# A four-layer graph network on one core: three small transposes taken from the TensorE stream to DMA, transposes of the first and last graphs taken the other way, two layers scheduled a round later

## The chip, the cores and the metric

The kernel runs on one core of a Trainium2 chip. The metric is the device time of one execution in microseconds (us), from the first instruction to the last. The kernel before takes 2822.43 us, the median of 3 runs (2820.94 to 2826.75). In the profile PE is TensorE's matmul, PEld its weight load, DVE is VectorE, ACT is ScalarE, POOL is GpSimd and SP is SyncE, whose queue issues all DMA here.

## The reference

There are 64 graphs of 256 nodes with 256 features, all in float32. Each graph goes through four layers, each followed by `x = layernorm(x + layer(x, adj))`; the graphs don't touch each other.

```python
# layer 0: 4 heads of 64, sigmoid attention, normed by degrees
att = sigmoid(einsum('bhxd,bhyd->bhxy', q, k) * scale)
adj_h = adj_matrix[:, None] * att
deg = sum(adj_h, axis=-1)
dis = where(deg > 0, deg ** (-0.5), 0.0)
A = dis[..., :, None] * adj_h * dis[..., None, :]
Y = layernorm(A @ X) * ln_g + ln_b
# layer 1: 8 heads of 32, softmax attention masked by adj > 0
out = (softmax(where(adj > 0, q @ k.T / sqrt(HD), NEG)) @ v) @ Wo + bo
# layer 2: agg = epsilon * x + adjacency @ x; hidden width 1024
h = agg @ W1 + b1
h = silu(h * rsqrt(mean(h ** 2) + eps) * rms_weight)
out = h @ W2 + b2
# layer 3: additive attention
e = leaky_relu(s1[:, :, None] + s2[:, None, :], 0.2)      # s1 = Wh @ a1, s2 = Wh @ a2
h_prime = softmax(where(adj > 0, e, NEG)) @ Wh
out = gelu(layernorm(h_prime) * gamma + beta)
```

## The kernel before

A graph's 256 nodes are two blocks of 128 partitions. `graph` (L238) lists the operations of one graph through all four layers, each with an engine, a cost in ns, what it reads and what it writes; nothing is issued there. `Plan.order` (L94) then lays the operations of all 64 graphs out in one order for the five engines: it keeps a clock for each engine, takes the operation that can start earliest (ties go to the one due first) and gives out tile slots as it goes. `emit` (L714) issues them in that order, so the order on each engine is fixed beforehand, and each engine works its own list in order.

Several graphs are in flight at once. `turn` (L249) gives every ACT function that needs a table (sigmoid, exp, silu, gelu) a place: layer l of graph b belongs to round b + ROUND[l], with ROUND = 0, 2, 5, 7 (L31). The last graphs are cut off at the last graph's number, 63, plus TAIL[l], with TAIL = 0, 2, 3, 5 (L32). An operation with a turn may not go before its turn; loads may go up to AHEAD = 14 quarter rounds (L29) before they are due. All other operations may go as soon as they are ready. Tiles are of six kinds with fixed numbers of slots (SLOTS, L33): "s" is half a K words in each partition in SBUF, "c" a small SBUF tile, "p" a PSUM bank, "h" a scratch buffer in DRAM.

Transposes are done in two ways. `transpose` and `transposed` (L258, L266) use PE against an identity: four 128x128 transposes into PSUM, followed by a copy on ACT (`copy`, L297). `far_transposed` (L271) uses DVE for the 32x32 blocks and two DMA hops through a DRAM scratch ("far") to put the blocks in place. The large ones already go through DRAM: layer 1's exponentials, two heads at a time (L521 transposes blocks, L523 writes, L525 reads them back as eT in four parts), layer 0's result yT (L478) and layer 3's input xT3 (L628). PE does x1 and layer 3's e (L492, L656).

Three small transposes are done by PE, each as two 128x128 transposes into PSUM:

- L457, layer 0: the degrees. L449 puts the sums of the four heads in rows, ACT copies them (L452), and L457 turns them so that a partition holds its own node's degrees. DVE and POOL make `dis` of them (L461 to L463), which scales v (L467) and later y (L482).
- L606, layer 2: 1/rms. L601 (POOL) leaves one number to a node in a column; L606 turns it into a row repeated on all partitions, which eight DVE operations (L609) multiply into the hidden layer.
- L646, layer 3: the source terms s2, a column of v3, turned into a row repeated on all partitions, which the two Prelu of L650 (ACT) read. L646 carries layer 3's turn for exp.

Of the kernel before, what the change touches and what calls it, by code (L numbers as in the profile page):

```python
# [11 lines left out]
OP = mybir.AluOpType  # L12
# [13 lines left out]
DMA_KB, DMA_SEEN = 4, 1900  # L26

WORDS = {"s": 516, "d": 1024, "b": 2048, "c": 32, "p": 512, "h": 1024}
AHEAD = 14  # L29

ROUND = 0, 2, 5, 7  # L31
TAIL = 0, 2, 3, 5  # L32
SLOTS = {"s": 42, "d": 10, "b": 3, "c": 72, "p": 8, "h": 8}  # L33


# [39 lines left out]
class Plan:  # L75
# [9 lines left out]
    def op(self, engine, cost, fn, w=(), r=(), turn=None, mode="full", after=None, size=0):  # L85
        pair = lambda x: x if isinstance(x, tuple) else (x, None)
        w, r = [pair(x) for x in w], [pair(x) for x in r]
        op = Op(engine, cost, fn, w, r, self.graph, turn, mode, after, size)
        op.table = turn is not None and engine == "ACT"
        if op.table:  # L90
            self.turns[turn] = self.turns.get(turn, 0) + 1
        self.ops.append(op)
# [145 lines left out]
def graph(plan, nc, c, t, out, b):  # L238
# [10 lines left out]
    def turn(layer, func):  # L249
        return 4 * min(b + ROUND[layer], plan.graphs - 1 + TAIL[layer]) + func  # L250
# [20 lines left out]
    def far_transposed(src, name, in_order=True):  # L271


        eb, far, dst = Value("s", "eb"), Value("h", "far", 4), Value("s", name, 4)
        op("DVE", 635, lambda: dve.transpose(
            eb.t.rearrange("p (b g i) -> p g b i", b=4, i=32),
            src.t.rearrange("p (n k w) -> p k n w", n=2, k=2)), [eb], [src])
        if in_order:
            F = lambda a: far.t[:64].rearrange("(a z) (y w) -> a (z y) w", a=4, w=P)[a]
            for a in range(4):  # L280
                op("SP", 420, lambda a=a: nc.sync.dma_start(
                    F(a).rearrange("(b j) w -> j b w", b=4),
                    eb.t[32 * a:32 * a + 32].rearrange("j (b w) -> j b w", b=4)), [(far, a)], [eb], after=3000, size=64)
            for a in range(4):
                op("SP", 420, lambda a=a: nc.sync.dma_start(
                    dst.t.rearrange("q (g a i) -> a q g i", g=4, a=4)[a],
                    F(a).rearrange("q (g i) -> q g i", g=4)), [(dst, a)], [(far, a)], after=4500, size=200)
            return dst
        op("SP", 420, lambda: nc.sync.dma_start(far.t[:, :512], eb.t), [(far, i) for i in range(4)], [eb], after=3000, size=256)
        for q in range(4):  # L290
            op("SP", 420, lambda q=q: nc.sync.dma_start(
                dst.t[32 * q:32 * q + 32].rearrange("j (a g) -> j a g", a=4),
                far.t[:, :512].rearrange("(a j) (b g) -> b j a g", a=4, b=4)[q]), [(dst, q)],
                [(far, i) for i in range(4)], after=4200, size=64)
        return dst

    def copy(ps, name):  # L297
        dst = Value("s", name, 2)
        op("ACT", 466, lambda: act.copy(dst.t, ps.t), [dst], [ps])  # L299
        return dst  # L300
# [126 lines left out]
    def fn(pss=pss):  # L427
        for hp in range(H0 // 2):
            for m in range(NB):
                for i in range(2):  # L430
                    s = slice(i * HD0, (i + 1) * HD0)
                    pe.matmul(two(pss[2 * hp + i])[:, m, :], two(kT)[s, hp, m * P:(m + 1) * P], two(qT)[s, hp, :],  # L432
                              start=True, stop=True)
# [16 lines left out]
    op("PE", PE_MM, fn, [ps], added, mode="columns")  # L450
    deg = Value("s", "deg")
    op("ACT", 258, lambda ps=ps: act.copy(deg.t[:, :N], ps.t[:, :N]), [deg], [ps])  # L452
    pd = Value("p", "ps")

    def fn():
        for n in range(NB):
            pe.transpose(pd.t[:, n * P:(n + 1) * P], deg.t[:, n * P:(n + 1) * P], c.ident)  # L457
    op("PE", 2 * PE_TR, fn, [pd], [deg], mode="transpose")
    dp, dis = Value("c", "dp"), Value("c", "dis")
    D8 = lambda: pd.t[:, :N].rearrange("p (g k) -> p g k", k=32)[:, :, 0]  # L460
    op("DVE", 50, lambda: dve.tensor_scalar(dp.t[:, :8], D8(), TINY, None, op0=OP.max), [dp], [pd])  # L461
    op("POOL", 1610, lambda: pool.tensor_tensor(dp.t[:, :8], dp.t[:, :8], c.mhalf, OP.pow), [dp], [dp])  # L462
    op("DVE", 83, lambda: dve.scalar_tensor_tensor(dis.t[:, :8], D8(), 0.0, dp.t[:, :8], op0=OP.is_gt, op1=OP.mult),  # L463
# [11 lines left out]
                    pe.matmul(two(ps)[i * HD0:(i + 1) * HD0, hp, :], two(v)[:, m, h * HD0:(h + 1) * HD0],  # L475
                              A(h)[:, m, :], start=(m == 0), stop=(m == NB - 1))
    op("PE", 4 * PE_MM, fn, [ps], [v, att], mode="columns")
    yb = far_transposed(ps, "yT", in_order=False)  # L478
    y = Value("s", "y", 2)
    for i in range(2):  # L480
        by = lambda ap, i=i: ap.rearrange("p g (i k w) -> p g i k w", i=2, k=2)[:, :, i]
        op("DVE", 345, lambda y=y, i=i, by=by: dve.tensor_tensor(  # L482
            by(y.t.rearrange("p (g d) -> p g d", g=4)), yb.t.rearrange("p (i k g w) -> p i g k w", i=2, k=2, g=4)[:, i],
            dis.t[:, :8].rearrange("p (g i) -> p i g", i=2)[:, i, :, None, None].to_broadcast([P, 4, 2, 32]), OP.mult),
            [y], [yb, dis])
    mv, m = stats(y)
    affine(y, mv, m, c.g0, lambda n, xb=xb: two(xb)[:, n, :], [xb])
    x = normed(y, "x1")
# [14 lines left out]
    for hq in range(H1 // 4):  # L503
        pss = [Value("p", "ps", 2) for _ in range(4)]

        def fn(hq=hq, pss=pss):
            for n in range(NB):
                for i in range(4):
                    s = slice(i * HD1, (i + 1) * HD1)
                    pe.matmul(two(pss[i])[:, n, :], two(qT1)[s, hq, n * P:(n + 1) * P], two(kT1)[s, hq, :],  # L510
                              start=True, stop=True)
        op("PE", 2 * PE_MM, fn, pss, [qT1, kT1], turn=turn(1, EXP), mode="rows")
        for pair in range(2):


            e, eb, far, eT = Value("d", "e", 4), Value("d", "eb"), Value("h", "far"), Value("d", "eT", 4)
            for i in range(2):
                softmax(pss[2 * pair + i], negmask, HD1 ** -0.5, e,
                        lambda n, i=i, e=e: e.t[:, 256 * (2 * i + n):256 * (2 * i + n + 1)],
                        lambda n, i=i: 2 * i + n, r, lambda n, h=4 * hq + 2 * pair + i: 2 * h + n, turn(1, EXP))  # L520
            op("DVE", 1155, lambda e=e, eb=eb: dve.transpose(eb.t.rearrange("p (b g i) -> p g b i", b=4, i=32),  # L521
                                                             e.t.rearrange("p (g b i) -> p g b i", b=4, i=32)), [eb], [e])
            op("SP", 420, lambda eb=eb, far=far: nc.sync.dma_start(far.t, eb.t), [far], [eb], after=3500, size=512)  # L523
            for q in range(4):
                op("SP", 420, lambda far=far, eT=eT, q=q: nc.sync.dma_start(  # L525
                    eT.t[32 * q:32 * q + 32].rearrange("j (a g) -> j a g", a=4),
                    far.t.rearrange("(a j) (b g) -> b j a g", a=4, b=4)[q]), [(eT, q)], [far], after=4000, size=128)
            eTs.append(eT)


    def fn():
        for hq in range(H1 // 4):
            for m in range(NB):
                for i in range(4):
                    h = 4 * hq + i
                    pe.matmul(two(av)[i * HD1:(i + 1) * HD1, hq, :], two(v1)[:, m, h * HD1:(h + 1) * HD1],  # L536
                              eTs[h // 2].t.rearrange("p (a h n k i) -> p h k n a i", a=4, h=2, n=2, k=2)[:, i % 2, m],
                              start=(m == 0), stop=(m == NB - 1))
    op("PE", 4 * PE_MM, fn, [av], [v1, *eTs], mode="columns")

    op("DVE", 180, lambda: dve.reciprocal(r.t[:, :16], r.t[:, :16]), [r], [r])
    ps = Value("p", "ps")
# [56 lines left out]
    rs = Value("c", "rs")  # L599
    op("DVE", 50, lambda ps=ps: dve.tensor_scalar(rs.t[:, :NB], ps.t[:, :NB], 1e-6, None, op0=OP.add), [rs], [ps])  # L600
    op("POOL", 700, lambda: pool.tensor_tensor(rs.t[:, :NB], rs.t[:, :NB], c.mhalf[:, :NB], OP.pow), [rs], [rs])  # L601
    pr = Value("p", "pr")

    def fn():
        for n in range(NB):
            pe.transpose(pr.t[:, n * P:(n + 1) * P], rs.t[:, n:n + 1].to_broadcast([P, P]), c.ident)  # L606
    op("PE", 2 * PE_TR, fn, [pr], [rs], mode="transpose")
    for j in range(HB):
        op("DVE", 391, lambda j=j: dve.scalar_tensor_tensor(  # L609
            Hb(j)[:, 0], Hb(j)[:, 0], c.r2.t[:, j:j + 1], pr.t[:, :N], op0=OP.mult, op1=OP.mult), [(hT, j)], [(hT, j), pr, c.r2])  # L610
# [14 lines left out]
    x = normed(plus(ps, xb), "x3")  # L625


    xT3 = far_transposed(x, "xT3")  # L628
    v3 = Value("s", "v3", 2)
    V3 = lambda: v3.full.rearrange("p (n c) -> p n c", n=2)  # L630
    s1 = lambda n: V3()[:, n, D:D + 1]
    for n in range(NB):
# [6 lines left out]
        op("PE", 2 * PE_MM + 4, fn, [ps], [xT3, c.w3])  # L639

        op("ACT", 260, lambda ps=ps, n=n: act.copy(V3()[:, n, :], ps.t[:, :D + 2]), [(v3, n)], [ps])
    ps2 = Value("p", "ps2")

    def fn():
        for n in range(NB):
            pe.transpose(ps2.t[:, n * P:(n + 1) * P], V3()[:, n, D + 1:D + 2].to_broadcast([P, P]), c.ident)  # L646
    op("PE", 2 * PE_TR, fn, [ps2], [v3], turn=turn(3, EXP), mode="transpose")
    e = Value("s", "e3", 2)
    for n in range(NB):
        op("ACT", 360, lambda n=n: act.activation(two(e)[:, n, :], ps2.t[:, :N], AF.Prelu, bias=s1(n), alpha=0.2),  # L650
           [(e, n)], [ps2, v3])
    negmask = masked(load("adj3", "adj"))
    r3 = Value("c", "r3")
    softmax(e, negmask, 1.0, e, lambda n: two(e)[:, n, :], lambda n: n, r3, lambda n: n, turn(3, EXP))
# [96 lines left out]
```

## Time and profile before

| engine | busy us | share of the span | instructions |
|---|---|---|---|
| PE | 2752.3 | 97% | 17092 |
| PEld | 2189.6 | 78% | 17092 |
| DVE | 2494.3 | 88% | 7757 |
| ACT | 2131.5 | 75% | 5054 |
| POOL | 585.8 | 21% | 902 |

The profiled span is 2823.4 us. The chain that ended last lies on PE for 87% of it, on DVE for 5%, ACT 3%, DMA 2%. The 16 DMA engines are busy for 59.2% with the queue that SP feeds, and move 479.40 MB in all. A busy time is the union of the records of an engine; a mean in ns is the length of one record. Records of PE overlap, so the time that an instruction takes from the stream is read from start to start in the timeline. A matmul of 128x256 in float32 is two instructions, a transpose is one.

### The profile page before, as it was taken

Reading aid. Unit: us, or ns where it says so; the run is one execution under the profiler, and the core shown is the slowest. Engines: PE = TensorE matmul, PEld = TensorE weight load, DVE = VectorE, ACT = ScalarE, POOL = GpSimd, SP = SyncE. Lnnn points to the kernel's source line nnn. Section 1 sums busy time; section 2 is a strip of 40 time slices with the busy share of each in tenths; the row PEclk is TensorE's granted clock in tenths of the full one; section 3 lists DMA queues with packets and bytes.
Section 4 is the critical chain, followed back from the end, with each engine's and each line's share of the span. In section 5 each row is a group of like instructions: output and inputs, shape, how many; then the busy total and the mean of one; then the engine's idle time right before and its main releaser. Section 6 shows DMA issues by size and latency. Waiting matters only on the chain.

```text
span 2823.4 us, 55149 instructions
## 1 busy us (share of the span) xinstructions
PE 2752.3 (97%) x17092; PEld 2189.6 (78%) x17092; DVE 2494.3 (88%) x7757; ACT 2131.5 (75%) x5054; POOL 585.8 (21%) x902
## 2 busy tenths in 40 slices
PE   8899999999999999999999999999999999999996
PEld 6667777887787878788878878778787778777784
DVE  5788898989899998998899989899989989899975
ACT  3767787778688777877777777878768877686774
POOL 1011211212222222212212212222212221212111
PEclk9999999999999999999999999999999999999998
DMA  4857476646466646665576556556556647475641
GB/s 142 252 151 196 152 202 180 187 134 192 127 193 199 197 135 200 192 179 148 155 192 180 172 163 183 171 167 187 174 149 183 198 141 201 125 194 153 181 123 41
DMA packets 558613, 479.40 MB, mean 170 GB/s; under 512 B 184304, under 2 KB 516976, under 8 KB 558320
## 3 DMA queue, kind: packets, MB, share of 16 engines
q1 hardware_dynamic: 558320, 475.87, 59.2%
q8 instruction: 137, 2.24, 0.4%
q14 instruction: 156, 1.28, 0.2%
HBM read 290.60 MB, written 185.07 MB: 168 GB/s over the span
## 4 chain that ended last, share of the span: by engine, by line
PE 87%; DVE 5%; ACT 3%; DMA 2%; SPq 1%; issue 1%; POOL 0%; DVEq 0%; POOLq 0%; ACTq 0%
PE ps L622 15%; PE ps L308 15%; PE ps L319 14%; PE ps L579 14%; PE ps L510 4%; PE ps L432 4%; PE ps L567 4%; PE ps L637 4%; PE ps L475 3%; PE av L536 3%; PE ps L263 2%; ACT e L400 1%; PE ps L449 1%; DVE e L395 1%; DVE st L333 1%
## 5 line engine op out<-in xcount | busy, mean ns | idle before, releaser
L400 ACT ACTIVATE e<-e,low 128x256 f32<-128x256 f32 x1152 | 575.7, 501 | 73.5 <-DVE low L395 69.8
L622 PE MATMUL ps<-w,hT 128*128 128x256 f32 x2048 | 480.6, 382 | 4.2 <-ACT hT L613 4.2
L579 PE MATMUL ps<-aggT,w 128*128 128x256 f32 x2048 | 470.8, 382 | 2.8 <-ACT aggT L299 1.4
L345 POOL TENSOR_SCALAR mv<-mv 128x2 f32<-128x2 f32 x384 | 123.0, 320 | 1624.8 <-DVE mv L335 1074.0
L579 PEld LDWEIGHTS ps<-aggT,w 128*128 128x128 f32 x2048 | 382.4, 190 | 69.2 <-issue 8.6
L622 PEld LDWEIGHTS ps<-w,hT 128*128 128x128 f32 x2048 | 381.3, 190 | 67.6 <-issue 10.5
L395 DVE CUSTOM_DVE_ANT_0 e<-ps,adj 128x256 f32<-128x256 f32 x1024 | 361.7, 420 | 33.5 <-PE ps L510 32.5
L521 DVE STREAM_TRANSPOSE eb<-e 128x1024 f32<-128x1024 f32 x256 | 310.5, 1225 | 4.7 <-ACT e L400 4.0
L346 POOL TENSOR_TENSOR mv<-mv,mhalf 128x2 f32<-128x2 f32 x384 | 307.7, 801 | 32.0
L584 ACT ACTIVATE hT<-ps,b 128x256 f32<-128x256 f32 x512 | 225.8, 473 | 97.0 <-PE ps L579 66.6
L360 ACT ACTIVATE x<-y,mv 128x256 f32<-128x256 f32 x384 | 216.2, 599 | 61.3 <-DVE mv L356 53.2
L333 DVE BATCH_NORM_STATS2 st<-y 128x6 f32<-128x256 f32 x640 | 242.3, 412 | 1.4
L400 ACT ACTIVATION_READ_ACCUMULATOR e<-e,low 128x1 f32 x1152 | 220.8, 192 | 0.0
L609 DVE SCALAR_TENSOR_TENSOR hT<-hT,r,pr 128x256 f32<-128x256 f32 x512 | 207.3, 474 | 7.0 <-PE pr L606 6.6
L590 DVE TENSOR_TENSOR sq<-sq 128x512 f32<-128x512 f32 x192 | 130.5, 680 | 48.1 <-ACT sq L587 47.0
L438 DVE TENSOR_TENSOR att<-att,adjT 128x512 f32<-128x512 f32 x256 | 165.7, 678 | 5.6 <-ACT att L436 5.5
L587 ACT ACTIVATE sq<-hT 128x512 f32<-128x512 f32 x256 | 163.1, 637 | 2.0 <-DMA far<-eb 0.6
L510 PE MATMUL ps<-kT,qT 32*128 32x256 f32 x2048 | 152.0, 404 | 1.0 <-ACT kT L299 1.0
L462 POOL TENSOR_TENSOR dp<-dp,mhalf 128x8 f32<-128x8 f32 x64 | 109.2, 1707 | 202.7 <-DVE dp L461 175.4
L436 ACT ACTIVATE att<-ps 128x512 f32<-128x512 f32 x256 | 132.3, 603 | 25.0 <-PE ps L622 18.6
L613 ACT ACTIVATE hT<-hT 128x1024 f32<-128x1024 f32 x128 | 129.8, 1051 | 19.5 <-DVE hT L609 17.0
L308 PE MATMUL ps<-x0T,w_q 128*128 128x256 f32 x512 | 132.1, 392 | 7.2 <-DMA x0T<-in_xT 7.2
(108 smaller groups left out, 5526.7 us busy)
## 6 DMA issues: line engine op xcount, KB each, us to landing
far<-eb SPq DMA_DIRECT2D x256, 512.0 KB, 3.5
eT<-far SPq DMA_DIRECT2D x1024, 128.0 KB, 3.9
adj<-in_adj SPq DMA_DIRECT2D x128, 256.0 KB, 4.7
x0T<-in_xT SPq DMA_DIRECT2D x64, 256.0 KB, 3.5
adjT<-in_adjT SPq DMA_DIRECT2D x64, 256.0 KB, 4.4
x<-in_x SPq DMA_DIRECT2D x64, 256.0 KB, 4.8
adj<-in_adjT SPq DMA_DIRECT2D x64, 256.0 KB, 5.3
far<-eb SPq DMA_DIRECT2D x64, 256.0 KB, 2.7
```

Of the source, the lines that this page charges most:

```text
L308: pe.matmul(two(ps)[:, o, :], w.t[:, k, o * P:(o + 1) * P], two(xT)[:, k, :], start=(k == 0), stop=(k == DB - 1))
L319: pe.matmul(two(ps)[:, n, :], two(xT)[:, k, n * P:(n + 1) * P], w()[:, k, :], start=(k == 0), stop=(k == DB - 1))
L333: op("DVE", 328, lambda n=n: dve.bn_stats(st.t[:, 6 * n:6 * n + 6], two(src)[:, n, :]), [(st, n)], [(src, n)])
L346: pool.tensor_tensor(m()[:, :, 2], m()[:, :, 2], c.mhalf[:, :NB], OP.pow)
L360: op("ACT", 492, lambda n=n: act.activation(two(dst)[:, n, :], two(src)[:, n, :], AF.Identity, bias=m()[:, n, 0:1], scale=m()[:, n, 2:3]), ...
L395: op("DVE", 345, lambda n=n: dve.tensor_tensor_reduce(out=E(n), in0=two(logits)[:, n, :], in1=two(negmask)[:, n, :], scale=-scale, scalar= ...
L400: op("ACT", 491, lambda n=n: act.activation(E(n), E(n), AF.Exp, bias=low.t[:, n:n + 1], scale=-1.0, accum_out=r.t[:, col(n):col(n) + 1]), ...
L510: pe.matmul(two(pss[i])[:, n, :], two(qT1)[s, hq, n * P:(n + 1) * P], two(kT1)[s, hq, :], start=True, stop=True)
L521: op("DVE", 1155, lambda e=e, eb=eb: dve.transpose(eb.t.rearrange("p (b g i) -> p g b i", b=4, i=32), e.t.rearrange("p (g b i) -> p g b i" ...
L579: pe.matmul(two(ps)[:, i, :], c.w2_1.t[:, k, (j + i) * P:(j + i + 1) * P], two(aggT)[:, k, :], start=(k == 0), stop=(k == DB - 1))
L584: op("ACT", 357, lambda ps=ps, i=i, j=j: act.activation(Hb(j + i)[:, 0], two(ps)[:, i, :], AF.Identity, bias=c.b2_1.t[:, j + i:j + i + 1]) ...
L622: pe.matmul(two(ps)[:, n, :], Hb(j)[:, 0, n * P:(n + 1) * P], c.w2_2.t[:, j, :], start=(j == 0), stop=(j == HB - 1))
```

## The change

The three small transposes leave PE. The degrees are written by DMA from the rows that hold them into a DRAM scratch, and read back element by element, one DMA for each block of nodes, into a small SBUF tile. 1/rms and the source terms go through a new helper, `spread_row`: a DMA writes the column into one row of a DRAM scratch, and a second reads this row into all 128 partitions of an SBUF tile. Seven DMA issues to a graph are added for six PE transposes. The results now lie in SBUF, not PSUM. As the transposes of the source terms carried layer 3's turn, the first Prelu carries it now.

The other way round, PE transposes replace the hops through DRAM where few graphs are in flight: NEAR = 1, 1, 3 gives yT of layer 0 for the first graph, the exponentials of layer 1 for the first graph, and xT3 for the last three graphs to PE, with copies on ACT.

Layers 2 and 3 of a graph come one round later (ROUND 6 and 8 for 5 and 7), the tail of layer 3 is a round shorter (TAIL 4 for 5), and loads are let in half a round later (AHEAD 12 for 14). The purpose is to free the PE stream of small work and to leave the longer way through DRAM time to land.

```diff
-AHEAD = 14
-
-ROUND = 0, 2, 5, 7
-TAIL = 0, 2, 3, 5
+AHEAD = 12
+NEAR = 1, 1, 3
+
+ROUND = 0, 2, 6, 8
+TAIL = 0, 2, 3, 4
...
+    def spread_row(src, v, name):
+
+        far, dst = Value("h", "far"), Value("s", name)
+        row = lambda: far.t[0:1, :N]
+        op("SP", 420, lambda: nc.sync.dma_start(row().rearrange("o (n p) -> (o p) n", n=NB), src()), [far], [v],
+           after=2600, size=24)
+        op("SP", 420, lambda: nc.sync.dma_start(dst.t[:, :N], row().to_broadcast([P, N])), [dst], [far], after=2600, size=128)
+        return dst
...
-    pd = Value("p", "ps")
-
-    def fn():
-        for n in range(NB):
-            pe.transpose(pd.t[:, n * P:(n + 1) * P], deg.t[:, n * P:(n + 1) * P], c.ident)
-    op("PE", 2 * PE_TR, fn, [pd], [deg], mode="transpose")
+    far, pd = Value("h", "far"), Value("c", "pd", 2)
+    op("SP", 420, lambda far=far: nc.sync.dma_start(far.t[:H0, :N], deg.t[0:97:32, :N]), [far], [deg], after=2200, size=8)
+    for n in range(NB):
+        op("SP", 420, lambda far=far, n=n: nc.sync.dma_start(
+            pd.t[:, n * H0:(n + 1) * H0], far.t[:H0, n * P:(n + 1) * P].rearrange("h p -> p h")), [(pd, n)], [far],
+            after=2600, size=48)
...
-    yb = far_transposed(ps, "yT", in_order=False)
...
+    if b < NEAR[0]:
+        ps = transposed(copy(ps, "yT"))
...
+    else:
+        yb = far_transposed(ps, "yT", in_order=False)
...
+            if b < NEAR[1]:
+                eT = Value("d", "eT", 2)
+                for i in range(2):
...
+                    transpose(lambda ps=ps: two(ps), lambda e=e, half=half: half(e), ps, e)
+                    op("ACT", 466, lambda ps=ps, eT=eT, half=half: act.copy(half(eT), two(ps)), [(eT, i)], [ps])
...
-    pr = Value("p", "pr")
-
-    def fn():
-        for n in range(NB):
-            pe.transpose(pr.t[:, n * P:(n + 1) * P], rs.t[:, n:n + 1].to_broadcast([P, P]), c.ident)
-    op("PE", 2 * PE_TR, fn, [pr], [rs], mode="transpose")
+    pr = spread_row(lambda: rs.t[:, :NB], rs, "pr")
...
-    xT3 = far_transposed(x, "xT3")
+    xT3 = copy(transposed(x), "xT3") if b >= plan.graphs - NEAR[2] else far_transposed(x, "xT3")
...
-    ps2 = Value("p", "ps2")
-
-    def fn():
-        for n in range(NB):
-            pe.transpose(ps2.t[:, n * P:(n + 1) * P], V3()[:, n, D + 1:D + 2].to_broadcast([P, P]), c.ident)
-    op("PE", 2 * PE_TR, fn, [ps2], [v3], turn=turn(3, EXP), mode="transpose")
+    s2 = spread_row(lambda: V3()[:, :, D + 1], v3, "s2")
...
-        op("ACT", 360, lambda n=n: act.activation(two(e)[:, n, :], ps2.t[:, :N], AF.Prelu, bias=s1(n), alpha=0.2),
-           [(e, n)], [ps2, v3])
+        op("ACT", 360, lambda n=n: act.activation(two(e)[:, n, :], s2.t[:, :N], AF.Prelu, bias=s1(n), alpha=0.2),
+           [(e, n)], [s2, v3], turn=turn(3, EXP) if n == 0 else None)
```

More of the change, by code (lines that the diff above doesn't have):

```diff
@@ L452, in graph @@
     op("ACT", 258, lambda ps=ps: act.copy(deg.t[:, :N], ps.t[:, :N]), [deg], [ps])
-    pd = Value("p", "ps")
-    def fn():
-        for n in range(NB):
-            pe.transpose(pd.t[:, n * P:(n + 1) * P], deg.t[:, n * P:(n + 1) * P], c.ident)
-    op("PE", 2 * PE_TR, fn, [pd], [deg], mode="transpose")
+    far, pd = Value("h", "far"), Value("c", "pd", 2)
[4 more added lines that the diff above has]
+            after=2600, size=48)
     dp, dis = Value("c", "dp"), Value("c", "dis")
-    D8 = lambda: pd.t[:, :N].rearrange("p (g k) -> p g k", k=32)[:, :, 0]
+    D8 = lambda: pd.t[:, :8]
     op("DVE", 50, lambda: dve.tensor_scalar(dp.t[:, :8], D8(), TINY, None, op0=OP.max), [dp], [pd])
@@ L477, in graph @@
     op("PE", 4 * PE_MM, fn, [ps], [v, att], mode="columns")
-    yb = far_transposed(ps, "yT", in_order=False)
     y = Value("s", "y", 2)
[L480 to L485, printed above, removed]
+    if b < NEAR[0]:
+        ps = transposed(copy(ps, "yT"))
+        op("DVE", 602, lambda ps=ps, y=y: dve.tensor_tensor(by_head(y.t), by_head(ps.t), dis_b(), OP.mult), [y], [ps, dis])
+    else:
+        yb = far_transposed(ps, "yT", in_order=False)
+        for i in range(2):
+            by = lambda ap, i=i: ap.rearrange("p g (i k w) -> p g i k w", i=2, k=2)[:, :, i]
+            op("DVE", 345, lambda y=y, i=i, by=by: dve.tensor_tensor(
+                by(y.t.rearrange("p (g d) -> p g d", g=4)), yb.t.rearrange("p (i k g w) -> p i g k w", i=2, k=2, g=4)[:, i],
+                dis.t[:, :8].rearrange("p (g i) -> p i g", i=2)[:, i, :, None, None].to_broadcast([P, 4, 2, 32]), OP.mult),
+                [y], [yb, dis])
     mv, m = stats(y)
@@ L513, in graph @@
         for pair in range(2):
-            e, eb, far, eT = Value("d", "e", 4), Value("d", "eb"), Value("h", "far"), Value("d", "eT", 4)
+            e = Value("d", "e", 4)
             for i in range(2):
@@ L520, in graph @@
                         lambda n, i=i: 2 * i + n, r, lambda n, h=4 * hq + 2 * pair + i: 2 * h + n, turn(1, EXP))
+            if b < NEAR[1]:
+                eT = Value("d", "eT", 2)
+                for i in range(2):
+                    half = lambda v, i=i: v.t[:, 512 * i:512 * (i + 1)].rearrange("p (n c) -> p n c", n=2)
+                    ps = Value("p", "ps", 2)
+                    transpose(lambda ps=ps: two(ps), lambda e=e, half=half: half(e), ps, e)
+                    op("ACT", 466, lambda ps=ps, eT=eT, half=half: act.copy(half(eT), two(ps)), [(eT, i)], [ps])
+                eTs.append((eT, lambda i, m, eT=eT: eT.t.rearrange("p (h m c) -> p h m c", h=2, m=2)[:, i, m]))
+                continue
+            eb, far, eT = Value("d", "eb"), Value("h", "far"), Value("d", "eT", 4)
             op("DVE", 1155, lambda e=e, eb=eb: dve.transpose(eb.t.rearrange("p (b g i) -> p g b i", b=4, i=32),
@@ L527, in graph @@
                     far.t.rearrange("(a j) (b g) -> b j a g", a=4, b=4)[q]), [(eT, q)], [far], after=4000, size=128)
-            eTs.append(eT)
+            eTs.append((eT, lambda i, m, eT=eT: eT.t.rearrange("p (a h n k i) -> p h k n a i", a=4, h=2, n=2, k=2)[:, i, m]))
     def fn():
@@ L536, in fn @@
                     pe.matmul(two(av)[i * HD1:(i + 1) * HD1, hq, :], two(v1)[:, m, h * HD1:(h + 1) * HD1],
-                              eTs[h // 2].t.rearrange("p (a h n k i) -> p h k n a i", a=4, h=2, n=2, k=2)[:, i % 2, m],
+                              eTs[h // 2][1](i % 2, m),
                               start=(m == 0), stop=(m == NB - 1))
-    op("PE", 4 * PE_MM, fn, [av], [v1, *eTs], mode="columns")
+    op("PE", 4 * PE_MM, fn, [av], [v1, *(eT for eT, _ in eTs)], mode="columns")
     op("DVE", 180, lambda: dve.reciprocal(r.t[:, :16], r.t[:, :16]), [r], [r])
```

## Prediction

> **What bounds the kernel now.** I read the page's busy line first, then a table by stage, then the timeline of PE, then the queue of SP. The busy line:
>
> ```profile
> PE 2752.3 (97%) x17092; PEld 2189.6 (78%) x17092; DVE 2494.3 (88%) x7757; ACT 2131.5 (75%) x5054; POOL 585.8 (21%) x902
> ```
>
> PE is busy for nearly all of the span and DVE is 258 us below it. An average hides stages, so the table by stage (time, then busy time and instructions of PE, PEld, DVE, ACT, POOL, then clock, DMA share, GB/s):
>
> ```profile
> 0.00:80.00 80.00, 67.39 (x378) 51.39 (x378) 48.89 (x136) 36.08 (x79) 11.66 (x21) 0.98 0.45 138
> 80.00:160.00 80.00, 68.54 (x411) 48.10 (x412) 61.99 (x176) 46.07 (x119) 9.13 (x11) 0.89 0.89 253
> ...
> 240.00:2500.00 2260.00, 2251.58 (x14108) 1799.96 (x14107) 2054.21 (x6402) 1760.11 (x4181) 489.10 (x742) 1.00 0.61 174
> ...
> 2760.00:2823.00 63.00, 35.49 (x144) 27.65 (x142) 37.04 (x126) 28.23 (x57) 11.98 (x23) 0.79 0.16 39
> ```
>
> From 240 to 2500 us PE is idle for 8.4 us of 2260. With 17092 / 64 = 267 instructions of PE to a graph, that stretch holds 52.8 graphs, 42.8 us each; DVE works 38.9 us of these and ACT 33.3. So the middle is bound by PE. The ends are not: PE is idle 24.1 us in the first 160 and 27.5 us in the last 63, at a lowered clock in part.
>
> A busy time of PE is no price of an instruction, since records overlap. The timeline of PE in the middle gives prices from start to start:
>
> ```profile
> 1439.22 1.97 PE L579 MATMUL ps<-aggT,w 128*128 128x256 f32 x8
> 1441.03 0.38 PE L606 MATMUL pr<-ident,rs 128*128 128x128 f32 x2
> 1441.24 0.38 PE L457 MATMUL ps<-ident,deg 128*128 128x128 f32 x2
> 1441.46 0.27 PE L543 MATMUL ps<-ident,r 128*16 128x128 f32 x1
> 1441.57 5.35 PE L579 MATMUL ps<-aggT,w 128*128 128x256 f32 x24
> 1446.76 0.59 PE L622 MATMUL ps<-w,hT 128*128 128x256 f32 x2
> ```
>
> A pair of transposes delays what follows by 0.21 to 0.22 us, 0.11 each, with no extra cost on the way in from L579 or back to it (24 of L579 take 5.19 us, 0.216 each). The groups by form say how many there are:
>
> ```profile
> L606 PE MATMUL pr<-ident,rs 128*128 128x128 f32 x128 | 26.0, 284 | 2.2 <-POOL rs L601 1.7
> L646 PE MATMUL ps<-ident,v 128*128 128x128 f32 x128 | 25.2, 280 | 2.9 <-ACT v L641 2.9
> L457 PE MATMUL ps<-ident,deg 128*128 128x128 f32 x128 | 24.6, 278 | 0.3 <-ACT deg L452 0.3
> ```
>
> **What the Trainium skill says.** "TensorE: Matmul & The Clock Gate", Part 4 (PE-mode transpose), puts a transpose at about 275 ns in a kernel. The trace agrees as a record (278 to 284 ns), but the slot that it occupies in the stream is 0.11 us, and that is what a removal returns. "DMA: Bandwidth & Descriptors", Rules for kernel authors, says a strided last dimension becomes one descriptor per element; here each half of the degrees becomes 512 pieces of 4 bytes. The nearest rows of before are L285, 512 pieces of 128 bytes, and one load of a bias column, 256 pieces of 4 bytes. The same page, Anatomy of one DMA, says that any wait is done by the issuing sequencer before dispatch. The trace agrees: the waits of the queue on SP are charged to single issue lines.
>
> **The change part by part.** *Removed.* L457, L606 and L646: 3 x 128 = 384 transposes x 0.109 us = 41.9 us, or 0.65 us to a graph. In the middle all of it is on the path that sets the end. Idle time of PE ahead of the three is 5.4 us in all by the groups; I count 3 of it as gone. Three PSUM tiles to a graph go too; PE shows almost no wait for a tile there, so zero.
>
> *Added on SP.* Seven issues to a graph: one to write the degrees out and two to read them back, two for 1/rms, two for the source terms. Prices of the nearest transfers (KB each, median us from issue to landing):
>
> ```profile
> eT<-far SPq DMA_DIRECT2D x1024, 128.0 KB, 3.9
> ...
> rb<-far SPq DMA_DIRECT2D x512, 32.0 KB, 2.0
> ...
> xT<-far SPq DMA_DIRECT2D x256, 64.0 KB, 2.6
> ...
> far<-rT SPq DMA_DIRECT2D x64, 8.0 KB, 2.8
> ...
> b_q<-in_L_gnn_bq SPq DMA_DIRECT2D x1, 1.0 KB, 5.2
> ```
>
> The write of the degrees is like far<-rT, 2.8. The element-wise ones I bound by rb, 2.0, below and by b_q above, 5.2, which was loaded in the crowded start; I take 2.6 to 3, since L285 (xT) has as many pieces. The broadcast of a row to 128 partitions has eT's size: 2.6 to 3.9, take 3.5. With two issues each chain is then some 6 to 7 us long where a pair of transposes with its write-out took about 0.5. In the middle that is hidden: layers 0 to 1 and 2 to 3 stay two rounds apart, 85 us, and layer 2 gets a third round more after layer 1. SP now issues 49 times to a graph at a median of 0.43 us, 21 us of 42.8; seven more at 0.43 to 0.62 make 24 to 25 of 42. DMA share: two broadcasts of 128 KB add 0.26 MB to 479.4 / 64 = 7.5 MB a graph, 3.5%; 1536 small pieces cost at least little and at most the mean packet of before, 0.592 x 16 x 2823 / 558320 = 48 ns, which is 1536 x 48 / 16 = 4.6 us of 42. So 0.61 becomes 0.63 to 0.75. No bound.
>
> *Waits added.* SP waits in order. These are its longest waits now (us in total, times, longest):
>
> ```profile
> SPq L523 <- DVE eb L521: 170.9, 84, 10.5
> SPq L281 <- DVE eb L275: 140.8, 30, 18.8
> SPq L289 <- DVE eb L275: 90.5, 22, 17.1
> ```
>
> An issue that waits for the ACT copy of the degrees, for POOL's 1/rms or for v3 holds every load and every eT behind it, and the second hop of each chain waits for the first to land. Behind the results stand DVE (L461; the eight of L609, 8 x 0.47 = 3.8 us of its queue) and ACT (the Prelu at L650), both in order. SP has about 18 us of spare time to a graph and DVE about 3.2 after the change (42.1 - 38.9), so short waits drown, but not all: I charge 0.1 us of PE idle to a graph, 7 us; bounds 0 and 0.4 us (26 us).
>
> *PE's own transposes.* Layer 0 of graph 0: 4; layer 1 of graph 0: 4 pairs x 8 = 32; layer 3 of the last three: 12. These 48 x 0.109 = 5.2 us of PE and 12 ACT copies x 0.59 = 7.1 us lie where both engines idle, so zero as work. In return graph 0 is spared these hops of the chain that ended last (start us, us, what):
>
> ```profile
> 83.70 4.95 DMA far<-eb
> 88.67 5.00 DMA eT<-far
> ```
>
> 10 us of latency in layer 1, and some 5 in layer 0, where the degrees' new chain gives back about as much. AHEAD 14 to 12 and a round more before layers 2 and 3 also let their loads come later; by the timeline of SP the second weight of layer 2 (1 MB) is issued at 100.6 us, where DMA is at 0.89. Against that, one more round of filling has layers 0 and 1 alone. I take 8 us off the start; bounds -20 and +8.
>
> *The end.* There is one round fewer (68, not 69), with five graphs in the last layer 3 in place of three, and one table cycle less in a row. But the last graph trades xT3's hops (2 x about 2.5 us) for the source terms' (about 6). I take 4 us off; bounds -15 and +10.
>
> Sum: 2822.4 - 41.9 - 3 + 7 - 8 - 4 = 2772.5, say 2772.
>
> **Rivals.** *Half is lost to waits* (chance 0.20): SP's queue comes a little late with eT and loads, 0.4 us of PE idle to a graph: 2772 + 19 = 2791, and to 2806 if the ends gain nothing. For it: SP already waits in order all the time, and no row shows small pieces at this rate. Against: eT is needed a round later. *The ends gain more* (0.15): they hold 51.6 us of idle and a lowered clock; a further 25 off gives 2747. For it: graph 0's latency and DMA at 0.89. Against: the five last graphs end in a run of DVE work, busy 37.04 of the last 63 us already. *Slower: DVE becomes the bound* (0.10). If each of the three chains makes DVE or ACT stand for 1.7 us, DVE's 38.9 becomes 44 us a graph, above 42.8: 64 x 1.2 = 77 us, 2822 + 77 - 12 = 2887; half of that wait leaves about 2825 to 2835. For it: DVE has only 3.2 us to a graph to spare, and 1/rms stands ahead of eight of its operations. Against: the plan puts other graphs' work before them, and DVE waits little for DMA today.
>
> **How the numbers follow.** The forecast has 0.55. The three cases below 2816 have 0.90 together; some of the second falls short, so faster 0.87, same 0.04, slower 0.09. The range from 2742 to 2806 leaves out most of the slower case and the tip of the third.
>
> **What would show it.** In the profile after, the three groups of pairs must be gone, PE's count near 17092 - 384 + 48 = 16756, and the middle 42.1 us to a graph with PE still above 99% busy there. If PE's idle between 240 and 2500 rises by tens of us with DMA landings (pd, pr, s2) as releasers, the waits were underpriced. DMA in 80 to 160 should fall below 0.89 and PE's busy there rise. Medians to landing above 5 us for the element-wise reads, or a stretch of DVE at 99%, would make the prediction wrong.

## The result, and the profile after

The changed kernel takes 3531.77 us (median of 4 runs, 3526.13 to 3542.26) against 2822.08 us before: ratio 1.2515, 95% interval 1.2482 to 1.2548. It is 710 us slower, where 50 us less was forecast.

The busy line of the page after:

```profile
PE 2977.0 (84%) x16756; PEld 2295.1 (65%) x16756; DVE 2487.8 (71%) x7748; ACT 2131.5 (60%) x5062; POOL 584.2 (17%) x902
```

PE issues 16756 instructions, the number that was forecast, yet is busy 225 us longer. DVE and ACT do the same work as before in a longer span. Nothing became an engine's bound; everybody waits. The table by stage (time, then busy time and instructions of PE, PEld, DVE, ACT, POOL, then clock, DMA share, GB/s):

```profile
80.00:160.00 80.00, 72.83 (x489) 54.66 (x488) 67.52 (x203) 57.21 (x157) 10.57 (x12) 0.96 0.72 208
...
240.00:3240.00 3000.00, 2560.82 (x14510) 1975.64 (x14508) 2157.80 (x6728) 1852.56 (x4402) 508.48 (x776) 0.92 0.64 142
```

The start went as the prediction said: in 80 to 160 us DMA falls from 0.89 to 0.72 and PE's busy time rises from 68.54 to 72.83. The middle did not. Without the 48 transposes of the ends there are 16708 / 64 = 261.1 instructions to a graph, so 14510 are 55.6 graphs, 54.0 us each where before took 42.8. PE is idle for 439 us of 3000 and runs at a granted clock of 0.92. DMA moves 142 GB/s for 174 at a share of 0.64 for 0.61: busier, and moving less. The shares look alike because the graph got longer: 0.64 x 54.0 = 34.6 us of DMA time to a graph, where before took 0.61 x 42.8 = 26.1. The chain that ended last shows whose waits these are (first by engine, then by line):

```profile
DMA 36%; PE 24%; DVE 12%; ACT 12%; issue 10%; SPq 5%; POOL 1%; DVEq 0%; ACTq 0%; POOLq 0%
DMA far<-v 9%; DMA far<-rs 7%; DMA far<-eb 5%; PE ps L318 5%; PE ps L329 4%; ACT e L410 4%; PE ps L603 4%; DMA eT<-far 3%; DMA pr<-far 3%; PE ps L641 3%; SPq L573 2%; PE ps L485 2%; PE ps L524 2%; DMA s<-far 2%; DVE hT L628 2%
```

PE has gone from 87% of the chain to 24%, DMA from 2% to 36%. At the head stand far<-v and far<-rs, the first hops of `spread_row`, which write the column of source terms and that of 1/rms into a DRAM row. Two waits of the compute engines for the second hops (us in total, times, longest) answer to that:

```profile
ACT e L664 <- DMA s<-far: 359.4, 47, 15.4
...
DVE hT L628 <- DMA pr<-far: 260.3, 44, 10.6
```

The page after has no landing times, but the packed trace holds the signals that each transfer gives as it lands. Read from the issue to the last of its 16 signals, the median is 9.4 us for far<-v and 10.3 for far<-rs, 5.0 and 4.9 for the hops that read them (s and pr), 2.8 for the reading of the degrees (pd), and 5.8 for layer 1's far<-eb, which took 3.5 before. (Three of 64 far<-v and twelve of 64 far<-rs lack some of their signals and are left out.) One place of the queue on SP (start us, us, instruction) shows when a hop could follow on the one before it:

```profile
1421.15 0.36 SPq L302 DMA_DIRECT2D far<-v  x1
1421.61 0.42 SPq L256 DMA_DIRECT2D adj<-in_adjT  x1
1429.27 0.34 SPq L304 DMA_DIRECT2D s<-far  x1
1430.41 0.34 SPq L547 DMA_DIRECT2D far<-eb  x1
1431.34 0.37 SPq L302 DMA_DIRECT2D far<-rs  x1
1431.82 0.45 SPq L547 DMA_DIRECT2D far<-eb  x1
1432.33 0.43 SPq L256 DMA_DIRECT2D x0T<-in_xT  x1
1441.43 0.33 SPq L549 DMA_DIRECT2D eT<-far  x1
1443.76 0.33 SPq L304 DMA_DIRECT2D pr<-far  x1
```

From far<-v to the hop that reads it are 8.1 us, in which SP issues one other DMA. And the far<-eb of 1430.41, a transfer that existed before and has nothing to do with the row, lets its eT go only after 11.0 us. So there are two suspects: the waits for the row, and something that the row does to its neighbours.

### The profile page after: what moved, and what is told of

Same layout as the page of the kernel before. It is cut to its first block, busy times and chain, and to the rows that moved or that the text cites. A ratio compares the mean times of both kernels' runs of the same rounds, so it can differ in the third digit from the quotient of the medians.

```text
span 3527.9 us, 54720 instructions
## 1 busy us (share of the span) xinstructions
PE 2977.0 (84%) x16756; PEld 2295.1 (65%) x16756; DVE 2487.8 (71%) x7748; ACT 2131.5 (60%) x5062; POOL 584.2 (17%) x902
## 4 chain that ended last, share of the span: by engine, by line
DMA 36%; PE 24%; DVE 12%; ACT 12%; issue 10%; SPq 5%; POOL 1%; DVEq 0%; ACTq 0%; POOLq 0%
DMA far<-v 9%; DMA far<-rs 7%; DMA far<-eb 5%; PE ps L318 5%; PE ps L329 4%; ACT e L410 4%; PE ps L603 4%; DMA eT<-far 3%; DMA pr<-far 3%; PE ps L641 3%; SPq L573 2%; PE ps L485 2%; PE ps L524 2%; DMA s<-far 2%; DVE hT L628 2%
## 5 line engine op out<-in xcount | busy, mean ns | idle before, releaser
L603 PE MATMUL ps<-aggT,w 128*128 128x256 f32 x2048 | 503.3, 400 | 74.9 <-ACT rT L569 60.5
L641 PE MATMUL ps<-w,hT 128*128 128x256 f32 x2048 | 526.4, 407 | 1.8 <-ACT hT L632 1.8
L603 PEld LDWEIGHTS ps<-aggT,w 128*128 128x128 f32 x2048 | 397.6, 199 | 157.5 <-ACT rT L569 66.6
L641 PEld LDWEIGHTS ps<-w,hT 128*128 128x128 f32 x2048 | 410.3, 206 | 74.4 <-issue 12.3
L664 ACT ACTIVATE e<-s,v 128x256 f32<-128x256 f32 x128 | 64.9, 515 | 513.7 <-DMA s<-far 359.4
L405 DVE CUSTOM_DVE_ANT_0 e<-e,adj 128x256 f32<-128x256 f32 x128 | 53.4, 420 | 291.0 <-ACT e L664 290.9
L264 PE MATMUL ps<-ident,x 128*128 128x128 f32 x268 | 67.5, 361 | 164.8 <-ACT x L370 163.8
L329 PE MATMUL ps<-w_l,x0T 128*128 128x256 f32 x512 | 144.2, 432 | 61.5 <-ACT kT L309 61.5
L560 PE MATMUL av<-eT,v 128*32 128x256 f32 x2048 | 151.5, 434 | 51.2 <-DVE qT L510 45.2
L524 PE MATMUL ps<-kT,qT 32*128 32x256 f32 x2048 | 182.8, 442 | 12.3 <-ACT kT L309 7.4
```

Of the source, the lines that this page charges most:

```text
L329: pe.matmul(two(ps)[:, n, :], two(xT)[:, k, n * P:(n + 1) * P], w()[:, k, :], start=(k == 0), stop=(k == DB - 1))
L405: op("DVE", 345, lambda n=n: dve.tensor_tensor_reduce(out=E(n), in0=two(logits)[:, n, :], in1=two(negmask)[:, n, :], scale=-scale, scalar= ...
L603: pe.matmul(two(ps)[:, i, :], c.w2_1.t[:, k, (j + i) * P:(j + i + 1) * P], two(aggT)[:, k, :], start=(k == 0), stop=(k == DB - 1))
L641: pe.matmul(two(ps)[:, n, :], Hb(j)[:, 0, n * P:(n + 1) * P], c.w2_2.t[:, j, :], start=(j == 0), stop=(j == HB - 1))
```

## The experiments

In these runs the plan is made anew for every edit, so the order of the whole kernel shifts; what this is worth shows below.

**Which part.** *Rows back on PE*: `pr` and `s2` by PE pairs again, the degrees on DMA, the schedule of the change.

```diff
-    pr = spread_row(lambda: rs.t[:, :NB], rs, "pr")
+    pr = Value("p", "pr")
+    ...            pe.transpose(pr.t[:, n * P:(n + 1) * P], rs.t[:, n:n + 1].to_broadcast([P, P]), c.ident)
```

> The changed kernel with 1/rms and the source terms turned into rows by PE again; the degrees stay on DMA, the schedule stays. Theory W (the 256 writes of 4 bytes into one DRAM row take 7 to 10 us to land and hold up the SP queue and what is behind it): about 2790 us, 2760 to 2830, since only 0.22 us of PE to a graph is still saved. Rival D (the element-wise reading of the degrees is the cause): stays above 3300. Rival S (the later rounds and AHEAD are the cause): stays above 3300.

Measured 2838.58 us, ratio 1.0053 (1.0032 to 1.0075). *Degrees back on PE*, rows on DMA:

> The changed kernel with the degrees transposed by PE again; both rows stay on DMA. Theory W: 3480 us, 3400 to 3540, as next to nothing of the loss is here. Rival D: about 2800. Rival S: stays above 3400.

Measured 3553.02 us, ratio 1.2584 (1.2555 to 1.2612). The rows make 693 of the 710 us; for the degrees, read back in 1024 pieces of 4 bytes, and the schedule together some 17 are left. The first kernel is 9 us above the interval given for it, the second 13; I come back to that.

**Size of the pieces.** A DVE transpose of 32x32 blocks turns the column first, so that each block's 32 values lie side by side in one partition; the same row is then written in 8 runs of 128 bytes. AHEAD is 11 here in place of 12.

```diff
-        op("SP", 420, lambda: nc.sync.dma_start(row().rearrange("o (n p) -> (o p) n", n=NB), src()), [far], [v],
-           after=2600, size=24)
+        op("DVE", 95, lambda: dve.transpose(
+            turned.t.rearrange("p (n i) -> p n i", n=NB), src()[:, :, None].to_broadcast([P, NB, 16])), [turned], [v])
+        for n in range(NB):
+            op("SP", 420, lambda n=n: nc.sync.dma_start(
+                far.t[0:1, n * P:(n + 1) * P].rearrange("o (k j) -> (o k) j", j=32), turned.t[16 * n:16 * n + 97:32, :32]),
+                [(far, n)], [turned], after=2600, size=4)
```

> The changed kernel, but the column is first turned by a DVE transpose of 32x32 blocks, so that the row is written in 8 runs of 128 bytes in place of 256 of 4 bytes; the same two hops, one more issue (AHEAD 11 for 12). Theory W with the size of the pieces as the cause: the row lands in 2 to 3 us and the kernel takes about 2780 us, 2750 to 2830. Rival H (any extra hop through DRAM that the SP queue has to wait for costs as much): stays above 3300. Rival S: stays above 3300.

Measured 2829.31 us, ratio 1.0018 (1.0011 to 1.0026). With the same row, the same two hops and one issue more to a row, 702 us are gone. It is how the row is written, not the way through DRAM; the blocks land in 2.1 us (median, to the last of the five signals that each gives). The time is at the upper end of what was expected, and no gain.

**Waits or neighbours.** One number in the changed kernel: the plan is told that the first hop lands after 9.0 us.

```diff
-           after=2600, size=24)
+           after=9000, size=24)
```

> The changed kernel with one number changed: the plan is told that the write of the row lands after 9.0 us and not after 2.6, so that it puts other work between the two hops. Theory Q (the loss is SP's in-order queue and in-order DVE and ACT standing at a landing that the plan had put too early): 2850 us, 2780 to 2950. Theory C (the 4-byte writes also clog the DMA engines, so that transfers beside them land late whatever the order): stays above 3150.

Measured 3452.63 us, ratio 1.2228 (1.2204 to 1.2253). The wait SPq L304 for far<-v falls from 342.2 to 40.0 us, and the kernel gets 79 us of 710 back. The readers still wait 275.7 us for s and 119.9 for pr: the plan still has the second hop land after 2.6 us, and it takes 5.1 and 3.9 (medians). So this one number is a small part; a plan with every landing right was not tried.

The next kernels have no reader of the rows at all: rows on PE as in the first experiment, and two *stray* writes to a graph of the same columns into a scratch that nothing reads.

```diff
+    def stray(src, v):
+        far = Value("h", "far")
+        op("SP", 420, lambda: nc.sync.dma_start(far.t[0:1, :N].rearrange("o (n p) -> (o p) n", n=NB), src()), [far], [v],
+           after=10000, size=24)
```

> The kernel with the rows on PE (run at 2838.6 us) plus the two 4-byte-piece writes of a DRAM row per graph, which nothing reads or waits for apart from the reuse of the scratch. Theory C (the writes hold up the transfers beside them): above 3100 us, as most of the loss stays with nobody waiting for them. Theory Q (the loss is in the waits for them): 2840 to 2880.

Measured 3290.99 us, ratio 1.1647 (1.1622 to 1.1672). Then the same with other DRAM addresses and nothing else: the order on every engine is the same in all five kernels of this kind. Words 2048 bytes apart, `far.t[:, 0:1024:512]`:

> The same with the 256 elements of each stray write put 2048 bytes apart in DRAM in place of side by side. Theory N (it is the writing of neighbouring 4-byte words of one DRAM row by many DMA engines at a time that is slow): 2840 to 2900 us. Theory P (any 4-byte piece written to DRAM costs as much, wherever it goes): within 3% of the stray row writes, so above 3050.

Measured 2826.36 us, ratio 1.0003 (0.9994 to 1.0012). Words 64 bytes apart:

> The stray writes again, with the 256 words 64 bytes apart in 16 KB (side by side took 3291 us, 2048 bytes apart 2826 us). Theory N1 (the cost comes from words that share a piece of DRAM of at most 64 bytes): 2820 to 2850 us. Theory N2 (it comes from words in the same page or bank, some KB): above 3000 us.

Measured 2825.76 us, ratio 1.0005 (0.9996 to 1.0015). The same 256 words, the same count of pieces and the same issues cost 465 us side by side and nothing at 64 bytes. Here is the same place of the plan in both, on SP's queue. Side by side:

```profile
1401.79 0.36 SPq L301 DMA_DIRECT2D far<-v  x1
1404.63 0.34 SPq L544 DMA_DIRECT2D far<-eb  x1
1405.01 0.43 SPq L256 DMA_DIRECT2D adj<-in_adjT  x1
1405.97 0.36 SPq L301 DMA_DIRECT2D far<-rs  x1
1406.57 0.34 SPq L544 DMA_DIRECT2D far<-eb  x1
1407.00 0.38 SPq L256 DMA_DIRECT2D x0T<-in_xT  x1
1414.41 11.25 SPq L546 DMA_DIRECT2D eT<-far  x8
```

and 64 bytes apart:

```profile
1213.96 0.36 SPq L301 DMA_DIRECT2D far<-v  x1
1216.81 0.34 SPq L544 DMA_DIRECT2D far<-eb  x1
1217.19 0.43 SPq L256 DMA_DIRECT2D adj<-in_adjT  x1
1218.14 0.36 SPq L301 DMA_DIRECT2D far<-rs  x1
1218.74 0.34 SPq L544 DMA_DIRECT2D far<-eb  x1
1219.18 0.38 SPq L256 DMA_DIRECT2D x0T<-in_xT  x1
1219.88 4.90 SPq L546 DMA_DIRECT2D eT<-far  x8
```

The first far<-eb releases its eT after 9.8 us in the one and 3.1 in the other, with nobody waiting for the row in either. The landing signals agree: far<-eb lands 9.7 and 3.0 us after its issue, and far<-v before it 10.6 and 1.5. The sums over the run say the same; waits of SP for far<-eb before issuing eT, side by side and then 64 bytes apart (us in total, times, longest):

```profile
SPq L546 <- DMA far<-eb: 286.4, 96, 10.1
```

```profile
SPq L546 <- DMA far<-eb: 55.2, 50, 3.0
```

The packets tell where the time goes. In the packet records of the two traces they add up to 32824 us side by side and to 27564 at 64 bytes, 329 us more for each of the 16 DMA engines. Of the 5261 us that this is, packets of 4 bytes make only 182: the mean packet of 1024 bytes goes from 59.8 to 72.4 ns, that of 4096 bytes from 175 to 208. By these records the delay lies on the transfers beside the row and hardly on the row's own pieces.

A part of the 465 us can still be a wait for the row, though nothing reads it. An issue here also waits until the transfer that had its semaphore or its scratch before has landed, and SP waits 52.0 us for far<-v and 71.1 for far<-rs in the run side by side. That is less than its waits for far<-eb; what it is worth in the kernel's time is not shown.

**How it grows.** Four words to 64 bytes, and two:

> Stray writes with the words 16 bytes apart, so four words share a 64-byte piece of DRAM (sixteen in the row: 3291 us; one: 2826 us). Theory R (the words that share a piece are written one after another, each a full round trip): a cost in proportion to the words behind the first, 3/15 of 465 us = 93, so about 2920 us, 2870 to 2980. Theory A (any sharing at all costs the whole): above 3150.

> The same with the words 32 bytes apart, two to a 64-byte piece. Theory R with a piece of 64 bytes: 1/15 of 465 us = 31, about 2857 us, 2840 to 2880. Theory R with a piece of 32 bytes: as 64 bytes apart, 2815 to 2835. Theory A: above 3150.

Measured 2835.45 us, ratio 1.0043 (1.0028 to 1.0057), and 2825.72 us, ratio 1.0005 (0.9997 to 1.0012). Both theories for the first are wrong. Four words to 64 bytes cost 10 us over one, not 93 and not everything; two cost nothing that can be measured, which theory R allowed for only with a piece of 32 bytes. The landing of the writes themselves (medians, in the same five kernels; side by side 12 of 64 far<-v and 8 of 64 far<-rs lack some of their signals and are left out) grows more evenly than the kernel's time:

| distance of the words, bytes | far<-v lands after, us | far<-rs lands after, us | kernel, us |
|---|---|---|---|
| 4 | 9.5 | 9.7 | 3290.99 |
| 16 | 3.2 | 3.4 | 2835.45 |
| 32 | 2.2 | 2.4 | 2825.72 |
| 64 | 1.9 | 2.4 | 2825.76 |
| 2048 | 2.2 | 2.5 | 2826.36 |

Against 64 bytes, far<-v takes 0.3 us longer with one word more in the same 64 bytes, 1.3 with three more and 7.7 with fifteen more: not far from proportion, as theory R has it, but in the landing and not in the kernel's time. A landing of 3 us costs this kernel 10 us in all, one of 10 us 465. What in DRAM or in the DMA makes the delay, and the size of the piece, stay open.

**Where the 42 us of PE are.** The kernel before, with the three pairs left out and constants read in their place (the degrees, 1/rms and source terms don't enter the output); then the same in the schedule of the change:

```diff
-    pr = Value("p", "pr")
-    ...
-    op("PE", 2 * PE_TR, fn, [pr], [rs], mode="transpose")
+    pr = c.g0
```

> The kernel before with the three pairs of PE transposes left out and nothing in their place: the degrees' reader, L609 and the two Prelu read constant tiles (so the degrees, 1/rms and source terms don't enter the output); every other operation runs. It measures the worth of the PE work that the change takes away, without any DMA. Theory F (PE bounds the middle, so its slots come back in full): 2822 - 42 - 3 = about 2777 us, 2765 to 2790. Rival M (engines run in order with two others nearly full, and a part comes back as stalls): 2795 to 2815.

> The same in the schedule of the change, with its own PE transposes at the ends: no pairs, no DMA for them, constants in their place (the three terms don't enter the output). Theory F: 2828 (the schedule alone) - 45 = about 2783 us. Rival M: 2800 to 2825. Against the blocks (2829) the difference is what the extra DMA costs even when written in blocks.

Measured 2794.69 us, ratio 0.9898 (0.9883 to 0.9913), and 2793.89 us, ratio 0.9897 (0.9882 to 0.9912). The first lies at the lower edge of the rival's range; the second lies between the two theories, 11 us above the one and 6 below the other's range. This is a measured ceiling: removing the pairs free of any price is worth 29 us, and 34 against the schedule alone, which follows. The stage from 240 to 2500 us of the first of the two:

```profile
240.00:2500.00 2260.00, 2242.36 (x13943) 1781.98 (x13941) 2069.73 (x6479) 1780.72 (x4228) 483.59 (x751) 1.00 0.61 175
```

At 16708 / 64 = 261.1 instructions to a graph these are 53.4 graphs, 42.3 us each for 42.8. Of 0.65 us of PE slots to a graph 0.47 come back, and PE's idle time in the stage has risen from 8.4 to 17.6 us.

*The schedule alone*, with all pairs on PE:

> All three small transposes on PE as before; only the schedule (rounds, tail, AHEAD) and PE's own transposes of the first and last graphs are changed. Theory E (the ends gain what the prediction took, 8 + 4 us): about 2811 us. Rival (the new schedule costs time, as the run with the rows on PE was 15 us above before although 14 us of PE were saved): 2835 to 2855.

Measured 2827.6 us, ratio 1.0006 (0.9997 to 1.0016): neither of the two. Its stage:

```profile
240.00:2500.00 2260.00, 2233.76 (x13957) 1778.11 (x13950) 2032.64 (x6337) 1746.48 (x4130) 488.73 (x734) 1.00 0.60 170
```

Without the 48 transposes of the ends there are 267 instructions to a graph as before, and 13957 are 52.26 graphs at 43.24 us. 64 x 43.24 leaves 2827.7 - 2767 = 60 us for the two ends, where before left 2823.4 - 64 x 42.78 = 85 (0.1 us to a graph is 6 us here). By this estimate the schedule shortens the ends by some 25 us and gives them back in the middle.

*The blocks with later landings in the plan* (3.5 us for the first hops, 4.5 for the second; AHEAD 12 again), and then with *the degrees on PE* as well:

> The kernel with the rows written in 128-byte blocks (run at 2829.3 us), with the plan told later landings for the small transfers (3.5 us for the first hops, 4.5 for the second, in place of 2.2 to 2.6). Theory L (what eats the 42 us of PE is DVE and ACT standing for pd, pr and s, 72 us in all in the middle): 2795 to 2810 us. Rival M (engines run in order close to full, and what PE no longer does turns into other stalls whatever the plan): 2820 to 2840.

> The rows in 128-byte blocks with the later landings in the plan, and the degrees transposed by PE as before. With the rows on PE, moving the degrees alone to DMA went from 2828 to 2839 us, 11 up although 14 us of PE were saved. Theory G (the 1024 pieces of 4 bytes of the degrees cost more than their transposes): 2805 to 2820 us, faster than both kernels. Rival M: 2825 to 2840.

Measured 2829.30 us, ratio 1.0010 (0.9999 to 1.0022), and 2851.63 us, ratio 1.0103 (1.0086 to 1.0120). The first is as its rival M had it. The waits that were to go are smaller in it but not gone. In the middle stage of the kernel with the blocks, DVE and ACT wait 17.5 us for pr, 35.5 for s and 22.0 for pd; with the later landings they wait for pd no more, and for the others:

```profile
DVE hT L631 <- DMA pr<-far: 27.2, 11, 3.8
...
ACT e L667 <- DMA s<-far: 20.8, 9, 4.0
```

The first has no pair on PE and takes as long as the schedule alone with all three. The second is above both of its theories, although its waits for pr and s come to 20 us in the middle stage; why is not shown. No kernel with the full function beat the one before.

**What a new order is worth.** The first experiment (2838.58) and the stray words at 64 bytes (2825.76) differ by 128 writes more in the second, and by the order that the plan makes of them; the one with more work is 13 us faster. So differences of some 10 us between kernels of different order are not put down here to the edit. That takes in the 11 us between the rows on PE and the schedule alone, which I had read as a price of the degrees when I wrote what I expected of the last kernel above.

## Why the prediction was wrong

**The step that failed** is the price under "Added on SP": "The element-wise ones I bound by rb, 2.0, below and by b_q above, 5.2 ...; I take 2.6 to 3". Both bounds came from transfers that *read* DRAM and write SBUF. The row's first hop writes 256 words side by side into DRAM, and no row of the page before did that. It lands after 9.4 and 10.3 us (medians), where 2.6 to 3 were taken; the broadcasts took 5.0 and 4.9 for 3.5. A chain is 14 to 15 us long and not 6 to 7. For the degrees' reading, which does read DRAM, the price was right: 2.8. The bound of the writes should have been called unknown from above.

**The second failing step** is the DMA share, 0.63 to 0.75, "No bound". The share came out within the range, 0.64, by luck: it is a share of 54.0 us to a graph. In DMA time the prediction allowed at most 0.75 x 42.1 = 31.6 us, and 34.6 were measured. The piece was priced at no more than the mean packet of before, 48 ns; by the packet records above, a piece of a row costs (32824 - 27564) us / 32768 = 161 ns more side by side than at 64 bytes, and nearly all of it on other transfers' packets. The prediction had no term for what a small write does to its neighbours. This is the larger term: 465 us with nobody reading the rows. The remainder of the 693 us, some 230, comes with readers that wait for the rows; the plan's landing time gives back 79 of it. That split holds for two kernels of different order.

**Waits added.** 0.1 us of PE idle to a graph was charged, 0.4 the upper bound; the middle lost 54.0 - 42.1 = 12 us to a graph against the forecast. The direction was named: ACT and DVE standing for s and pr in their queues, the third rival. Its size came from DVE's 3.2 us of slack and reached 2887 us. The delays fell on other transfers too, so that no engine became a bound at all. What stood against it, that DVE waits little for DMA today, had no force: what DVE waits for is what the change was about to change. The lowered clock, 0.92 in the middle, goes with the idle time of PE; it was not tried by itself.

**"In the middle all of it is on the path."** 41.9 + 3 us were to come back from the pairs; without any price in their place it is 28.8. A slot measured from start to start, 0.11 us, is what a transpose takes from the stream, but not "what a removal returns": here 0.47 of 0.65 us to a graph. With DVE at 0.91 of the middle and every queue in order, a part turning into other waits is the likely reason; it was not tried by itself.

**The ends.** -12 us were forecast, and the start did look as described. Measured alone, the schedule is at 1.0006 (0.9997 to 1.0016), as the middle loses what the ends gain. The 48 transposes at the ends were not tried alone.

Two sums of the rivals don't come out as written: 2791 us without a gain at the ends is 2803, not 2806, and half of the third rival's wait leaves DVE at about 41.5 us to a graph, below PE, which makes nothing slower. Neither bears on the outcome.

The Trainium skill, "DMA: Bandwidth & Descriptors", Specifications, says that below 512 bytes a transfer is not at line rate and does a read-modify-write. That would have been a warning, but it doesn't tell these cases apart: words of 4 bytes at 64 bytes' distance and runs of 128 bytes are below 512 as well, and cost nothing that the kernel's time shows. In these runs it is the distance to the neighbours in DRAM that decides.

## What to carry to other kernels

Before a column is laid out as a row through DRAM, turn it on chip so that it is written in longer runs: 8 runs of 128 bytes in place of 256 of 4 took this kernel from 3532 to 2829 us. (Words written 32 bytes apart or more cost nothing here either, but reading such a row back was not tried.) A DMA that nobody waits for can still be the slow one, and its mark is that unrelated transfers land late. The DMA share hardly moves, because the span grows with it, so look at DMA time per piece of work. Giving the suspect other addresses, in the same order, shows it. And measure what a removal is worth with nothing in its place before paying for it: the ceiling of this change was about 30 us.

## What the runs showed of the hardware that was not expected

Two writes to a graph of 256 words of 4 bytes, side by side in one DRAM row, cost this kernel 465 us (3290.99 against 2825.76 at 64 bytes' distance) with nobody reading them; the same words 32, 64 or 2048 bytes apart cost nothing that can be measured, and 16 bytes apart 10 us. Such a write lands after 9.5 us (median), at 64 bytes' distance after 1.9. While it is under way, other transfers of the same queue are held up: at one place a far<-eb of 512 KB lands after 9.7 us in place of 3.0. Whether transfers of another queue would be held up as well is not shown, as all DMA of this kernel goes through SP's.
